# A two-layer graph transformer on one core: products of the seven-product blocks at the head of the next chunk, attention steps spread anew, two weight sums at other chunks

## The chip, the cores and the metric

The kernel runs on one core of a Trainium2 chip. The metric is the device time of one execution in microseconds (us); lower is better. Engines: TensorE (PE) multiplies matrices, VectorE (DVE), ScalarE (ACT) and GpSimd (POOL) do the rest, SyncE (SP) and the other queues issue DMAs. Each engine works its own instructions in the order in which the kernel gives them out and waits for the others through semaphores.

## What is computed

Two layers, one after the other, over 2708 nodes with 512 features, 8 heads and a 0/1 adjacency matrix with some nine ones in a row, the diagonal included. Each layer is

```
q, k, v = h @ Wq.T + bq, h @ Wk.T + bk, h @ Wv.T + bv        # 8 heads of 64
scores  = where(adj + eye == 0, -1e9, q.k / 8);  attn = softmax(scores)
h1 = layer_norm(h + (attn @ v) @ Wo.T + bo)
h2 = layer_norm(h1 + relu(h1 @ W1.T + b1) @ W2.T + b2)       # 512 -> 2048 -> 512
```

All of it is in float32.

## The kernel before, in words

The nodes are sorted by their number of neighbours and cut into 22 tiles of 128 (the last has 20). A tile gathers the keys and values of its neighbours slot by slot instead of forming the full score matrix. Tiles go in pairs called blocks; there are 11, k = 0 to 10, and the last holds the tile of 20 rows.

A layer is a loop over blocks, and in each block a loop over the 16 **chunks** f of the hidden 2048 features. A chunk is four matmuls into a PSUM tile pf (8 records in the profile, since a float32 matmul is recorded twice) and a relu on ACT into ft (L1656). Between two chunks the generator yields, and the driver loop puts other work in this gap, always at the same f:

- f = 5 to 8, "behind" (`keys_values`): the pair of the block before is turned for the next layer. f = 5: transposes of both tiles z (tp, L1285) and their copies zT on ACT (L1290). f = 6 and 7: one tile's k and v projection each (L620), k evicted by DVE (L1723), v by ACT (L1728). f = 8: two scatters to DRAM by POOL.
- f = 10, 11, 12, "attended": the next block's attention result cx. f = 10: transpose of the first tile and its copy cT on ACT. f = 11: first tile's output projection o, then the transpose of the second tile. f = 12: the second tile's o. Each o is followed on DVE by the residual, the bias and a layer norm (L1447 to L1279; its reciprocal root, L1275, is on POOL).
- f = 15: transposes of both normed tiles h, copies hT on ACT, for the next block's first chunk.
- in every gap, last: `advance(pace[f])` adds pace[f] to a credit (held at 1.5 at most) and issues steps of the **attention** of tiles further on while the credit is above zero. A step takes one or two neighbour slots: on DVE a product with q (L1150), a reduction (L1156) and two operations of an earlier step (L1182, L1189), some 4.3 us together; on ACT two exponentials (L1169) and eight scalings (L1176); on POOL two gathers, three steps ahead. A tile's last step is followed by eight divisions on ACT (cx, L1220).

Blocks 2 to 9 of layer 0 multiply ft by W2 in **seven products instead of eight** (`feed_forward_by_seven`). Chunks 2j and 2j+1 make pair j. Four small DVE operations form sums of the pair's ft (`sums`, L1617 to L1620), and seven matmuls of 256 columns (`products`, L1635) use them and sums of the weights, which lie in DRAM (form_d) and come back pair by pair (`ask_forms`, L1602, on SP). `sums(j)` is given out in chunk 2j+2, `products(j)` in chunk 2j+5. After chunk 15: the last pair but one, the last two chunks of ft by the plain way (L1665, L1669), products(6), and then DVE combines the accumulators into z (L1687 to L1695) and norms both tiles. The next block follows.

The sums of the weights are formed once, in block 1, on DVE (`form`, L1584 to L1587, four operations for each of seven pairs, then three stores by SP) in the gaps of the chunks listed in FORMS. Forms 0 to 5 use the same three buffers, so each waits until the stores of the one before have landed; form 6 has buffers of its own.

Four things set waits around the change. pf has two PSUM buffers, so chunk f waits for the relu of chunk f-2. The sums have two buffers, so `sums(j)` waits for `products(j-2)`. ACT's queue is strict: a copy that waits for TensorE holds up the relus behind it. Transposes and projections share two further PSUM buffers.

Of the kernel before, what the change touches and what calls it, by code (L numbers as in the profile page):

```python
# [51 lines left out]
    (0.0,) * 4 + (0.85,) * 8 + (0.0,) * 2 + (0.8,) * 2,  # L52
    (0.75,) * 11 + (0.0,) * 2 + (0.9,) * 3,
)
PACE7 = (0.0,) * 3 + (0.75,) * 2 + (1.2,) * 4 + (0.75,) * 2 + (0.0,) * 2 + (0.85,) * 3
FORMED = 1
FORMS = (3, 5, 7, 9, 13, 14, 15)
PACE = (
    (0.0,) * 2 + (0.6,) * 3 + (1.2,) * 4 + (0.6,) * 2 + (0.0,) * 2 + (0.8,) * 3,
    (0.0,) * 2 + (0.82,) * 9 + (0.0,) * 2 + (1.0,) * 3,  # L60
# [423 lines left out]
def by_edges(ctx: ExitStack, tc: tile.TileContext, x, xT, adj, layers, out, redo):  # L484
# [780 lines left out]
    def norm(z, r, gain, shift, st=None):  # L1265

        if st is None:
            st = small.tile([P, 6], F32, tag="st", name="st")
            nc.vector.bn_stats(st[:r], z[:r])
        mv = small.tile([P, 2], F32, tag="mv", name="mv")  # L1270
        nc.vector.bn_aggr(mv[:r], st[:r])
        va = small.tile([P, 1], F32, tag="va", name="va")
        nc.vector.tensor_scalar(va[:r], mv[:r, 1:2], EPS, None, ALU.add)  # L1273
        rd = small.tile([P, 1], F32, tag="rd", name="rd")
        nc.gpsimd.tensor_tensor(rd[:r], va[:r], mhalf[:r], ALU.pow)  # L1275
        nc.vector.scalar_tensor_tensor(
            z[:r], z[:r], mv[:r, 0:1], gain[:r], ALU.subtract, ALU.mult
        )
        nc.vector.scalar_tensor_tensor(z[:r], z[:r], rd[:r], shift[:r], ALU.mult, ALU.add)  # L1279
# [14 lines left out]
    class Layer:  # L1294
# [310 lines left out]
        def feed_forward_by_seven(self, k, block, hs, hT):  # L1605

            J, W = NFC // 2 - 1, 2 * P
            L, R = slice(0, W), slice(W, DM)
            a0, a1 = (ps_a.tile([P, DM], F32, tag=f"a{i}", name=f"a{i}") for i in range(2))
            c0, c1 = (ps_s.tile([P, DM], F32, tag=f"c{i}", name=f"c{i}") for i in range(2))  # L1610
            fts = []
            base = 3 * J * (k - FORMED - 1)

            def sums(j):
                f0, f1 = fts[2 * j], fts[2 * j + 1]
                s = self.sums[j % 2]
                nc.vector.tensor_tensor(s[:, 0], f1[:, P:], f0[:, P:], ALU.add)  # L1617
                nc.vector.tensor_tensor(f0[:, P:], f0[:, :P], f0[:, P:], ALU.subtract)
                nc.vector.tensor_tensor(s[:, 1], s[:, 0], f0[:, :P], ALU.subtract)
                nc.vector.tensor_tensor(s[:, 2], f1[:, :P], s[:, 1], ALU.subtract)  # L1620

            def products(j):
                f0, f1, w, s = fts[2 * j], fts[2 * j + 1], self.w2[j], self.sums[j % 2]
                t2, t3, t4 = self.slots
                first, last = j == 0, j == J - 1
                for to, left, right, start, stop in (
                    (a1[:, L], f1[:, P:], t4, first, last),
                    (c0[:, R], s[:, 1], t2, first, False),
                    (c1[:, L], f0[:, P:], t3, first, False),
                    (c0[:, L], f0[:, :P], w[:, 0, L], False, last),  # L1630
                    (a0[:, L], f1[:, :P], w[:, 1, L], first, False),
                    (c1[:, R], s[:, 0], w[:, 0, R], False, last),
                    (a0[:, R], s[:, 2], w[:, 1, R], False, last),
                ):
                    nc.tensor.matmul(to, left, right, start=start, stop=stop)  # L1635
                self.ask_forms(base + min(3 * j + 6, 3 * J + 3 * (k < NB - 2)))
                if k == NB - 2:
                    self.form_back(j)

            self.ask_forms(base + 3)  # L1640
            for f in range(NFC):
                j = f // 2
                pf = ps_f.tile([P, DM], F32, tag="f", name="pf")
                for c in range(NC):
                    nc.tensor.matmul(  # L1645
                        pf[:, :W],
                        self.w1[j][:, c, f % 2 * P : f % 2 * P + P],
                        hT[:, c, :],
                        start=(c == 0),
                        stop=(c == NC - 1),  # L1650
                    )
                if f % 6 < 4:
                    ft = dn.tile([P, W], F32, tag="ft", name="ft", bufs=4)
                else:
                    ft = self.more_fts[f % 2]
                nc.scalar.activation(ft, pf[:, :W], AF.Relu, bias=self.b1[:, f : f + 1])  # L1656
                fts.append(ft)
                if f % 2 == 0 and j > 0:
                    sums(j - 1)
                if f % 2 and j > 1:  # L1660
                    products(j - 2)
                yield None
            for i in range(2):
                f, w = 2 * J + i, self.w2[J]
                nc.tensor.matmul(a0, fts[f][:, :P], w[:, i, :], start=False, stop=False)  # L1665
            for cols in (L, R):
                for i in range(2):
                    f, w = 2 * J + i, self.w2[J]
                    nc.tensor.matmul(  # L1669
                        a1[:, cols],  # L1670
                        fts[f][:, P:],
                        w[:, i, cols],
                        start=False,
                        stop=False,
                    )
            products(J - 1)
            zA, zB = hs
            u2 = dn.tile([P, W], F32, tag="ft", name="u2", bufs=4)
            u34 = dn.tile([P, DM], F32, tag="row", name="u34", bufs=3)

            def twice(t):
                return t.unsqueeze(1).to_broadcast([P, 2, W])

            def pair(t):
                return t.rearrange("p (two n) -> p two n", two=2)

            nc.scalar.copy(u2, c0[:, L])  # L1687
            nc.vector.tensor_tensor(zA[:, L], u2, zA[:, L], ALU.add)
            nc.vector.tensor_tensor(u2, c0[:, R], u2, ALU.add)
            nc.vector.tensor_tensor(pair(u34), pair(c1), twice(u2), ALU.add)  # L1690
            nc.vector.tensor_tensor(zB[:, R], c1[:, R], zB[:, R], ALU.add)
            nc.vector.tensor_tensor(zA, a0, zA, ALU.add)
            nc.vector.tensor_tensor(zB, a1, zB, ALU.add)
            nc.vector.tensor_tensor(zA[:, R], u34[:, R], zA[:, R], ALU.add)
            nc.vector.tensor_tensor(pair(zB), pair(zB), twice(u34[:, L]), ALU.add)  # L1695
            for z in hs:
                norm(z, P, self.g2, self.e2)
            yield list(hs)
# [110 lines left out]
    def advance(more):  # L1809

        nonlocal credit
        if not more:
            return
        credit = min(credit + more, 1.5)
        while credit > 0 and len(got) < CXB:
            cost = next(ahead, None)
            if cost is None:
                break
            credit -= cost
# [49 lines left out]
    for n in range(NL):  # L1869
# [47 lines left out]
        for k, block in enumerate(blocks):  # L1917
# [14 lines left out]
            for f, zs in enumerate(working):  # L1932
# [16 lines left out]
                if more and f == NFC - 1:  # L1949
                    finish(asking)  # L1950
                    hT = now.turned(blocks[k + 1], hs_next)
                advance((PACE7 if seven else (PACE if k else PACES)[n])[f])
                if f in (0, 3, 7, 9) and (f or k):
# [4 lines left out]
                if n > 0 and (k, f) == (0, 2):  # L1958
                    now.load_second(1, temp)
                if n == 0 and k == FORMED and f in FORMS:  # L1960
                    now.form(FORMS.index(f))
                if last and not more and f == 8:
# [108 lines left out]
```

## Time and profile before

| What | us |
|---|---|
| median of 3 runs (1845.54 to 1848.74) | 1846.1 |
| profiled execution, its own time | 1845.1 |
| its span (first to last instruction) | 1843.4 |
| stretch of the seven-product blocks | 393 to 1020 |

Busy time by engine in stretches of the span, one to a block (the blocks' work straddles the cuts a little):

| stretch, us | length | PE busy | DVE busy | ACT busy |
|---|---|---|---|---|
| 392.0 to 472.0 (block 2) | 80.0 | 74.15 | 68.82 | 37.87 |
| 472.0 to 550.9 | 78.9 | 76.50 | 68.03 | 42.38 |
| 550.9 to 627.2 | 76.3 | 75.74 | 68.71 | 41.46 |
| 627.2 to 707.2 | 80.0 | 77.26 | 68.56 | 44.70 |
| 707.2 to 783.6 | 76.4 | 76.27 | 67.23 | 42.38 |
| 783.6 to 862.9 | 79.3 | 77.04 | 68.06 | 44.23 |
| 862.9 to 939.2 | 76.3 | 75.26 | 70.03 | 42.02 |
| 939.2 to 1020.0 (block 9) | 80.8 | 78.34 | 49.57 | 31.32 |

How to read it: busy time of PE counts matmuls whose ends are modelled, so the idle time in front of each matmul is the better measure. The profile names for each idle time the engine that ended it. Granted clock is the share of full speed that TensorE was given.

### The profile page before, as it was taken

Reading aid. Unit: us, or ns where it says so; the run is one execution under the profiler, and the core shown is the slowest. Engines: PE = TensorE matmul, PEld = TensorE weight load, DVE = VectorE, ACT = ScalarE, POOL = GpSimd, SP = SyncE. Lnnn points to the kernel's source line nnn. Section 1 sums busy time; section 2 is a strip of 40 time slices with the busy share of each in tenths; the row PEclk is TensorE's granted clock in tenths of the full one; section 3 lists DMA queues with packets and bytes.
Section 4 is the critical chain, followed back from the end, with each engine's and each line's share of the span. In section 5 each row is a group of like instructions: output and inputs, shape, how many; then the busy total and the mean of one; then the engine's idle time right before and its main releaser. Section 6 shows DMA issues by size and latency. Waiting matters only on the chain.

```text
span 1843.4 us, 22524 instructions
## 1 busy us (share of the span) xinstructions
PE 1812.7 (98%) x6563; PEld 1164.1 (63%) x6563; DVE 1460.4 (79%) x2447; ACT 950.5 (52%) x3271; POOL 799.4 (43%) x745
## 2 busy tenths in 40 slices
PE   9999999999999999999999999999999999999998
PEld 4444466566767867777677644666666666666666
DVE  5996778888888889889985247977988897889853
ACT  4770445545555555555643204565655675566531
POOL 3234755534454454444531022444554554456302
PEclk9999999999999999999999999999999999999999
DMA  9997987756666675665742677835554564555300
GB/s 340 365 347 257 371 279 237 245 166 228 205 222 206 206 258 191 215 200 192 244 161 90 231 247 276 314 124 197 193 192 174 207 249 150 210 195 184 135 20 21
DMA packets 158063, 393.82 MB, mean 214 GB/s; under 512 B 17515, under 2 KB 60895, under 8 KB 157929
## 3 DMA queue, kind: packets, MB, share of 16 engines
q0 software_dynamic: 70608, 252.12, 40.0%
q1 hardware_dynamic: 77162, 118.55, 18.7%
q10 hardware_dynamic: 10158, 21.61, 3.1%
q8 instruction: 54, 0.88, 0.2%
q14 instruction: 81, 0.66, 0.1%
HBM read 338.78 MB, written 53.44 MB: 213 GB/s over the span
## 4 chain that ended last, share of the span: by engine, by line
PE 82%; DVE 9%; ACT 4%; issue 3%; POOL 2%; DMA 1%; POOLq 0%; SPq 0%; DVEq 0%
PE pf L1515 18%; PE a L1488 17%; PE k L620 8%; PE v L620 8%; PE q L620 8%; PE o L620 7%; PE pf L1645 5%; PE c L1635 4%; PE a L1635 2%; PE tp L1285 2%; ACT kv L1176 2%; DVE sc L1156 2%; DVE kv L1150 1%; POOL rd L1275 1%; DVE h L1279 1%
## 5 line engine op out<-in xcount | busy, mean ns | idle before, releaser
L1113 POOL DMA_INDIRECT kv<-kv_d,listed x420 | 519.9, 1238 | 287.9 <-issue 114.4
L1515 PE MATMUL pf<-hT,w 128*128 128x256 f32 (+1 forms) x1792 | 393.3, 367 | 0.1
L1515 PEld LDWEIGHTS pf<-hT,w 128*128 128x128 f32 x1792 | 323.7, 190 | 103.0 <-issue 63.9
L1488 PE MATMUL a<-w,ft 128*128 128x512 f32 x800 | 373.2, 592 | 0.0
L1176 ACT ACTIVATE kv<-kv,p 128x64 f32<-128x64 f32 x1232 | 311.0, 335 | 5.0
L1275 POOL TENSOR_TENSOR rd<-va,mhalf 128x1 f32<-128x1 f32 (+1 forms) x88 | 80.7, 917 | 533.5 <-DVE va L1273 533.4
L1150 DVE TENSOR_TENSOR kv<-kv,q 128x1024 f32<-128x1024 f32 (+1 forms) x222 | 256.9, 1157 | 14.3 <-DMA q<-q_d,ident_i 11.0
L1156 DVE TENSOR_REDUCE sc<-kv 128x16 f32<-128x1024 f32 (+1 forms) x222 | 257.9, 1162 | 7.6
L1645 PE MATMUL pf<-hT,w 128*128 128x256 f32 x1024 | 235.1, 382 | 9.5 <-ACT ft L1656 9.5
L1189 DVE TENSOR_TENSOR acc<-acc,kv 128x1024 f32<-128x1024 f32 (+2 forms) x178 | 205.3, 1154 | 32.9 <-ACT kv L1176 17.3
L1645 PEld LDWEIGHTS pf<-hT,w 128*128 128x128 f32 x1024 | 193.3, 191 | 47.6 <-issue 11.9
L1488 PEld LDWEIGHTS a<-w,ft 128*128 128x128 f32 x800 | 150.3, 190 | 113.1 <-issue 101.2
L1526 ACT ACTIVATE ft<-pf,b 128x256 f32<-128x256 f32 (+1 forms) x208 | 94.8, 458 | 197.8 <-PE pf L1515 197.6
L1169 ACT ACTIVATE p<-sc,listed 128x8 f32<-128x8 f32 x420 | 104.3, 297 | 161.7 <-DVE sc L1156 150.8
L620 PE MATMUL o<-wo,cT 128*128 128x512 f32 x336 | 151.0, 593 | 1.1 <-ACT cT L1290 1.1
L1182 DVE TENSOR_TENSOR kv<-kv,p 128x512 f32<-128x512 f32 (+1 forms) x178 | 123.3, 693 | 9.8 <-ACT p L1169 9.6
L620 PEld LDWEIGHTS o<-wo,cT 128*128 128x128 f32 x336 | 63.5, 190 | 74.7 <-issue 66.2
L1656 ACT ACTIVATE ft<-pf,b 128x256 f32<-128x256 f32 x96 | 44.6, 466 | 114.1 <-PE pf L1645 114.1
L745 DVE MAX8 tops<-code 128x8 f32<-128x247 f32 (+2 forms) x242 | 78.9, 400 | 27.2 <-ACT code L740 27.0
L1279 DVE SCALAR_TENSOR_TENSOR h<-h,rd,ln_b 128x512 f32<-128x512 f32 (+1 forms) x88 | 66.1, 751 | 43.2 <-POOL rd L1275 43.2
L1220 ACT ACTIVATE cx<-acc,su 128x64 f32<-128x64 f32 (+1 forms) x352 | 88.2, 333 | 14.6 <-DVE su L1212 8.9
L1447 DVE TENSOR_TENSOR h<-o,xb 128x512 f32<-128x512 f32 (+1 forms) x44 | 30.3, 689 | 79.7 <-PE o L620 63.1
(231 smaller groups left out, 2332.0 us busy)
## 6 DMA issues: line engine op xcount, KB each, us to landing
aj<-in_adj SPq DMA_DIRECT2D x42, 677.0 KB, 6.2
forms<-form_d SPq DMA_DIRECT2D x168, 128.0 KB, 3.8
kv_d<-kvs ACTq DMA_DIRECT2D x21, 512.0 KB, 7.1
xg<-in_xT SPq DMA_DIRECT2D x19, 512.0 KB, 8.2
w<-in_W SPq DMA_DIRECT2D x16, 512.0 KB, 6.5
kv<-kv_d,listed POOLq DMA_INDIRECT x420, 6.0
zT_d<-zT SPq DMA_DIRECT2D x22, 256.0 KB, 3.5
xb_d<-h SPq DMA_DIRECT2D x21, 256.0 KB, 5.2
```

The costliest lines, as they stand in the source:

```text
L620: nc.tensor.matmul(o[:r], xs(c), wm[:, c, :], start=(c == 0), stop=(c == NC - 1))
L1113: return nc.gpsimd.indirect_dma_start(out=to, out_offset=None, in_=table[:, :], in_offset=bass.IndirectOffsetOnAxis(ap=s, axis=0), bounds_ ...
L1150: nc.vector.tensor_tensor(kv[:r, :c, :DM], kv[:r, :c, :DM], self.q[:r].unsqueeze(1).to_broadcast([r, c, DM]), ALU.mult,)
L1156: nc.vector.tensor_reduce(self.sc[:r, s0 : s0 + c, :], kv[:r, :c, :DM].rearrange("p s (h d) -> p s h d", d=DK), AX.X, ALU.add,)
L1169: nc.scalar.activation(p[:r, s, :], self.sc[:r, s, :], AF.Exp, bias=minus[:r, g, s : s + 1])
L1176: nc.scalar.activation(to[:, i, hd], kv[:r, i, DM + h * DK : DM + (h + 1) * DK], AF.Copy, scale=p[:r, s0 + i, h : h + 1],)
L1182: nc.vector.tensor_tensor(to[:, 0, :].rearrange("p (h d) -> p h d", d=DK), kv[:r, 0, DM:].rearrange("p (h d) -> p h d", d=DK), p[:r, s0, : ...
L1189: nc.vector.tensor_tensor(self.acc[:r, :c, :], self.acc[:r, :c, :], kv[:r, :c, DM:], ALU.add)
L1488: nc.tensor.matmul(a[:r, cols], fts[f][:, c0 : c0 + r], self.w2[f // 2][:, f % 2, cols], start=(f == 0), stop=(f == NFC - 1),)
L1515: nc.tensor.matmul(pf[:, :w], self.w1[f // 2][:, c, f % 2 * P : f % 2 * P + P], hT[:, c, :w], start=(c == 0), stop=(c == NC - 1),)
L1635: nc.tensor.matmul(to, left, right, start=start, stop=stop)
L1645: nc.tensor.matmul(pf[:, :W], self.w1[j][:, c, f % 2 * P : f % 2 * P + P], hT[:, c, :], start=(c == 0), stop=(c == NC - 1),)
```

## The change

Three edits, all in layer 0:

```
-PACE7 = (0.0,) * 3 + (0.75,) * 2 + (1.2,) * 4 + (0.75,) * 2 + (0.0,) * 2 + (0.85,) * 3
+PACE7 = (0.0,) * 4 + (0.6,) + (1.3,) * 4 + (0.6,) * 2 + (0.0,) * 2 + (0.5, 0.8, 2.4)
 FORMED = 1
-FORMS = (3, 5, 7, 9, 13, 14, 15)
+FORMS = (3, 5, 7, 9, 11, 13, 15)
...
                 if f % 2 == 0 and j > 0:
                     sums(j - 1)
+                yield None
                 if f % 2 and j > 1:
                     products(j - 2)
-                yield None
```

- **Products.** `products(j)` is given out after the gap of chunk 2j+5 instead of ahead of it, just before the matmuls of chunk 2j+6. On TensorE the gap's work of chunks 5, 7, 9, 11, 13 and 15 therefore comes before the seven products. The requests for the weight sums (`ask_forms`) and, in block 9, the requests that bring W2 back move with it on SP's queue, past the stores of zT and z in that gap.
- **Pace.** In blocks 2 to 9 the attention's credit by chunk is 0 to 3: nothing (before: nothing up to 2, then 0.75), 4: 0.6 (0.75), 5 to 8: 1.3 (1.2), 9 and 10: 0.6 (0.75), 11 and 12: nothing, 13: 0.5, 14: 0.8, 15: 2.4, of which at most 1.5 is held (before 0.85 each).
- **Weight sums.** Form 4 moves from chunk 13 to 11 of block 1 and form 5 from chunk 14 to 13.

## The prediction

> **What bounds the kernel now.** First the page's busy times: TensorE is busy nearly throughout, so only its idle time can be won. Then who ended that idle time between 392 and 1021 us, where the blocks that the edit touches lie (columns: total us, times, longest).
>
> ```profile
> PE   1812.7 (98%) x6563; PEld 1164.1 (63%) x6563; DVE 1460.4 (79%) x2447; ACT 950.5 (52%) x3271; POOL 799.4 (43%) x745
> ```
>
> ```profile
> PE pf L1645 <- ACT ft L1656: 9.5, 7, 2.2
> PE c L1635 <- issue: 3.1, 1, 3.1
> PE k L620 <- ACT zT L1290: 2.8, 5, 0.6
> PE c L1635 <- DVE forms L1619: 1.0, 1, 1.0
> PE a L1635 <- DVE h L1559: 0.8, 1, 0.8
> ```
>
> That is 17.2 us in 15 waits. The start-to-start times of the tail matmuls (L1665) hold all losses: 386.5 (the first chunk of block 2 at 393.0, less the tail and seven products, 6.5), 470.3, 548.8, 625.5, 705.9, 781.5, 860.5, 937.5 and 1013.8. A block without a wait is 75.45: 16 chunks at 1.73, 7 times 3.02 for seven products, four k or v at 3.43, two o, 2.6 of transposes, 3.44 of tail, at the pitches that the timeline shows (block 6: 75.6); block 9, whose o of 20 rows takes 1.0, is 72.9. Above that lie 8.3, 3.1, 1.2, 5.0, 0.1, 3.5, 1.5 and 3.4 us for blocks 2 to 9: **26.1 us is all that these edits can win.**
>
> The commonest loss, block 3's, on TensorE and then ACT:
>
> ```profile
> 518.10 0.59 PE L1635 MATMUL a<-w,forms 128*128 128x256 f32 x2
> 520.03 1.99 PE L1645 MATMUL pf<-hT,w 128*128 128x256 f32 x8 [1.34 <-ACT ft L1656]
> 521.86 0.60 PE L1285 MATMUL tp<-ident,cx 128*128 128x128 f32 x4
> 522.83 2.00 PE L1645 MATMUL pf<-hT,w 128*128 128x256 f32 x8 [0.36 <-ACT ft L1656]
> ```
>
> ```profile
> 512.25 0.58 ACT L1728 COPY kvs<-v 128x512 f32<-128x512 f32 x1 [9.41 <-PE v L620]
> ...
> 517.62 2.00 ACT L1220 ACTIVATE cx<-acc,su 128x64 f32<-128x64 f32 x8
> 519.52 0.46 ACT L1656 ACTIVATE ft<-pf,b 128x256 f32<-128x256 f32 x1
> ```
>
> ACT's queue stands at the copy of the second v until TensorE ends it. Then come two steps (2.45 each), the divisions (1.92), and only then the relu of chunk 8, for which chunk 10 waits. Between that v and chunk 10 TensorE has 6.5 us of other work.
>
> **Products after the gap.** It adds no instruction, only order. In block time (0 is the first chunk, 10.35 the end of chunk 5):
>
> - *Chunk 7.* Both of the second k and v now precede products(1), so ACT's copy is released 3.02 us earlier against chunk 10: v ends at 31.4, chunk 10 stands at 40.9. ACT by rows: v copy 32.0, a step 34.4, relu 8 when its chunk ends, 36.6, a step and the divisions 41.0, relu 9 at 41.4. Chunk 10 needs relu 8 and chunk 11, at 43.1, relu 9: both in time. In blocks 5 and 6 a second step precedes relu 9 in the new order: 43.8, a wait of 0.7 each. 9.5 becomes 1.4.
> - *Chunk 5.* The transposes of z come before products(0), so zT has 3.0 us more before k asks: the 2.8 go. That the relu of chunk 4 no longer stands behind a step of chunk 3 (the pace) helps too.
> - *What is late next, at chunk 11.* o of the first tile loses the cover of products(3). Relu 10 follows a step, 44.2, then four copies cT of 0.26: 45.25. o could start at 44.8. It waits 0.4 to 0.6 in blocks 2, 3, 4 and 7; in 5 and 6 chunk 11's own wait covers it. In block 9 relu 9 stands behind two steps and the divisions of tile 0: 2.9 if they wait for DVE as the durations have it, 1.5 if not. I take 2.9, since DVE is the later queue there.
> - *At chunk 15* the transposes of h lose the same 3.02. h is normed 4.3 us after the second o (536.91 to 541.24); then come two chunks, products(4) and another: 8.2 us, still covered. Without that cover one norm chain, 4.3, would show.
> - *SP.* The weight sums of the last pair are asked for when the first matmul of products(5) frees a buffer; 6.46 us lie between that and products(6), as much as between products(4) and (5) before, where no wait shows. The page has 3.8 us to landing. zT and z are ready by then, so nothing waits behind their stores: nothing. If that cover went, each late load would be a wait of its lateness.
>
> **z at chunk 5: the price.** The transposes of z now meet DVE without products(0) ahead. z is ready 9.95 us after its first operation (476.07 to 486.02), itself due some 13.1 us after chunk 14's start. From the end of the second o DVE has: norm 4.3, 0.6 until products(4) frees the sums, sums 1.1, two full steps 8.6, the closing step with its tile's sums 4.2, about 0.8 waiting for ACT, z 9.95: 29.6. TensorE from there to the second transpose of z: chunk 1.73, products 3.02, two chunks 3.45, transposes 0.87, products 3.02, tail 3.44, products 3.02, six chunks 10.35, 0.44: 29.3. So they meet within half a microsecond: I put 0.45 each on blocks 5, 6 and 8, nothing on 4 and 7 (a one-slot step), nothing on 9. Block 3 pays 1.85, since in block 2 a fourth step stands behind the second o. The wait does not build up: the second o holds DVE again in every block. Products(0) itself moves 0.87 later while its sums stay, so the 1.0 of block 8 goes.
>
> **Weight sums sooner.** Before, products(0) of block 2 stood still at 405.06, and the page says "issue"; DVE's timeline has its sum (L1619) at 407.71, the end of block 1's norms. DVE idled before both o of block 1 (2.85 and 2.89 us) and waited 0.81 for the stores in the last forms. Form 4 (1.76) now falls into the second idle time, and the store has four chunks more: z and the sums come 2.55 earlier, at 404.65. The transposes, asked at 403.5, wait 0.9; the 3.88 go.
>
> **Pace.** Ten to eleven steps a block as before. The step at chunk 3 moves behind; what it costs is in the three steps before z above.
>
> [...] The waits have a second price. The windows after the two longest waits:
>
> ```profile
> 408.00:412.00 4.00, 3.90 (x11) 3.20 (x12) 3.86 (x8) 0.00 (x0) 3.08 (x4) 0.62 0.71 223
> 678.00:682.00 4.00, 3.76 (x10) 3.03 (x11) 3.83 (x7) 3.90 (x16) 2.46 (x3) 0.58 0.94 329
> ```
>
> The column before the last two is the granted clock: 0.62 after an idle 3.06 and 0.58 after 2.18, where the chunk took 3.43 instead of 1.89. After idles of 1.98 and 1.90 it stayed 1.00. These slow stretches are some 1.75 and 1.5 us, 3.3 of the 26.1. [...]
>
> **The sum.** New waits: 0.9 + 0.6 (block 2), 1.85 + 0.4 (3), 0.4 (4), 0.45 + 0.7 (5), 0.45 + 0.7 (6), 0.4 (7), 0.45 (8), 2.9 (9) = 10.2. Twelve restarts at 0.1 (eight records take 1.99 after a wait, 1.89 without): 1.2. Clock once: 1.5. One norm's reciprocal root kept behind gathers on POOL, as at 848.13 (1.59 idle instead of 0.45): 1.1. Together 14.0 against 26.1: **12 us won**. The profiled execution, 1845.1, becomes 1833; the median shown, 1.0 above it, 1834. The rest, from 1020 us on, is moved forward unchanged: layer 1 hangs on block 10's keys, and TensorE waits there for 2 us in all.
>
> Bounds: if z is on time everywhere and block 9 waits 1.5 without a clock loss, new losses are 5.5 and the time 1825.5. If POOL's 1.1 falls on all seven blocks and two idles cost clock, 7.7 and 3.0 more: 1845.
>
> **Rivals.**
>
> - *The wait moves, half the gain.* o at cT waits 1.5 in each block, not 0.4, because steps on ACT are stretched by exponentials that wait for DVE (8.6 us and 20.7 us of such waits now, on either side), and z some 0.4 more: 6 us less won, 1840. For it: both meetings above are within half a microsecond. Against: ACT is busy 42 of 76 us and idles 9 us before that v.
> - *Slower: z becomes the bound.* Should DVE be 2.5 us later at z than worked out in each of seven blocks, TensorE waits 17.5 us more at chunk 5, and these idles, at 2.5 to 3, cost 1.5 of clock each, 10.5: 1834 + 28 = 1862. It decides from about 1.5 us of lateness per block (10.5 takes the gain away). For it: DVE is busy 68 to 70 of 76 us, and 1.95 us of such lateness stood at 868.25 in block 7. Against: in six of eight blocks z waited for ACT's copy now, 0.2 to 1.3 us and 10.3 in the last, and the second o resets the queue.
> - *Only block 2 gains.* If the order of the products is hidden anyway, the 3.88, the clock after it and a little remain: 1840.5. Against: the waits for the relus are TensorE's own idle time, on the chain of waits.
>
> **How the numbers follow.** My forecast, 1834 with its own range 1829 to 1839: 0.68. Half the gain or block 2 only, about 1840: 0.24, of which a quarter lies above 1842.4. Slower: 0.08. Some 0.2% (3.7 us) is what a measurement tells from no change. Faster: 0.68 + 0.18 = 0.86; within: 0.06 and 0.01 of the last; slower 0.07. The range runs from 1828 to 1843, with 0.1 left above and a little below.
>
> **What would show it.** Right: no wait of pf on ft over 1 us; none of k on zT; waits of o on cT of about half a microsecond; transposes of z waiting for DVE by less than 2 us; products(0) of block 2 by about 406; the tail's start-to-start near 76.3; the stage ending near 1008. Wrong: z's transposes waiting 2 us or more in most blocks with windows of clock near 0.6, or the forms' loads ending waits of products(6).

## The result, and the profile after

| | before | after |
|---|---|---|
| median, us (range, 5 runs each) | 1846.7 (1845.5 to 1848.7) | 1836.6 (1834.3 to 1838.4) |
| ratio of times, 95% interval | | 0.9945 (0.993 to 0.9959) |
| profiled execution, its own time | 1845.1 | 1835.8 |
| its span | 1843.4 | 1834.1 |
| first chunk of block 2 to the tail of block 9 | 393.00 to 1013.78: 620.78 | 394.26 to 1004.77: 610.51 |

The last row is the measure used from here on, called **the stretch**: from the first record of L1645 of block 2 to the first of L1665 of block 9. It became 10.27 us shorter. That it began 1.26 later in this execution lies ahead of the blocks measured (TensorE waited 1.17 for DVE at 151 us, for one), and differs between the kept traces: 392.84 to 394.51. The change won 10 us, where 12 were predicted.

The busy times hardly tell the two kernels apart. The columns are busy us, share of the span and instructions:

```profile
PE 1809.1 (99%) x6563; PEld 1163.0 (63%) x6563; DVE 1458.5 (80%) x2447; ACT 948.7 (52%) x3271; POOL 798.9 (44%) x745
```

The waits of TensorE between 385 and 1015 us do (total us, times, longest). This is the whole list:

```profile
PE tp L1285 <- DVE h L1279: 3.9, 6, 1.6
PE pf L1645 <- ACT ft L1656: 3.8, 3, 2.2
PE o L615 <- ACT cT L1290: 2.4, 1, 2.4
PE a L1635 <- DMA forms<-form_d: 0.4, 1, 0.4
```

17.2 us of waits have become 10.5. The relus fell from 9.5 to 3.8, and k's waits for zT and those for the sums are gone. In their place stand the transposes of z, which now meet DVE at chunk 5, and one wait of o. Block 3 after, the place of the commonest loss before; ACT, then TensorE (start, us, instruction):

```profile
511.92 2.00 ACT L1220 ACTIVATE cx<-acc,su 128x64 f32<-128x64 f32 x8
513.83 0.45 ACT L1656 ACTIVATE ft<-pf,b 128x256 f32<-128x256 f32 x1
...
516.99 1.11 ACT L1290 ACTIVATE cT<-tp,bv 128x128 f32<-128x128 f32 x4
```

```profile
513.46 0.59 PE L1635 MATMUL a<-w,forms 128*128 128x256 f32 x2
513.89 1.89 PE L1645 MATMUL pf<-hT,w 128*128 128x256 f32 x8
515.62 0.60 PE L1285 MATMUL tp<-ident,cx 128*128 128x128 f32 x4
516.05 1.89 PE L1645 MATMUL pf<-hT,w 128*128 128x256 f32 x8
517.78 2.74 PE L620 MATMUL o<-wo,cT 128*128 128x512 f32 x6
```

The divisions still stand ahead of a relu, but the products now stand ahead of chunk 10 on TensorE, and no bracket follows either L1645: nothing waited. o, too, starts at 517.78 without a wait, while the four copies cT last until 518.10: its first matmuls do not wait for all four.

What the prediction did not have is in block 8. POOL, DVE and then TensorE (in brackets the idle time before, and who ended it):

```profile
882.33 1.75 POOL L1113 DMA_INDIRECT kv<-kv_d,listed  x1 [9.68 <-DVE acc L1189]
884.38 1.51 POOL L1113 DMA_INDIRECT kv<-kv_d,listed  x1 [0.30 <-issue]
886.19 0.99 POOL L1113 DMA_INDIRECT kv<-kv_d,listed  x1 [0.30 <-issue]
887.48 1.61 POOL L1113 DMA_INDIRECT kv<-kv_d,listed  x1 [0.30 <-issue]
889.40 1.00 POOL L1113 DMA_INDIRECT q<-q_d,ident_i  x1 [0.30 <-issue]
```

```profile
889.15 0.20 DVE L1212 RECIPROCAL su<-su 128x8 f32<-128x8 f32 x1
894.76 1.22 DVE L1150 TENSOR_TENSOR kv<-kv,q 128x1024 f32<-128x1024 f32 x1 [5.41 <-DMA q<-q_d,ident_i]
```

```profile
900.22 1.99 PE L1645 MATMUL pf<-hT,w 128*128 128x256 f32 x8 [2.24 <-ACT ft L1656]
```

Read upwards: chunk 11 waited 2.24 for the relu of chunk 9. On ACT that relu, at 899.72, stood behind the exponentials and scalings of a step, which began at 897.27 because DVE's product with q began at 894.76. DVE had been idle since 889.35, because the gather of q was issued at 889.40; and that gather stood on POOL behind four gathers of keys and values, the first of which had waited 9.68 us for a free buffer.

The granted clock fell once, to 0.50 for 3.41 us, around the end of the wait of o in block 9. (Columns: start and end, length, busy time of TensorE with its records, granted clock, DMA share, GB/s. A stretch of 4 us across the edge shows a mean, 0.68 from 980 to 984.)

```profile
978.05:981.46 3.41, 1.00 (x8) 1.00 0.00 0
981.46:984.88 3.42, 3.42 (x14) 0.50 0.02 5
```

### The profile page after: what moved, and what is told of

Its sections match the earlier page's. It is cut to its first block, busy times and chain, and to the rows that moved or that the text cites. A ratio compares the mean times of both kernels' runs of the same rounds, so it can differ in the third digit from the quotient of the medians.

```text
span 1834.1 us, 22527 instructions
## 1 busy us (share of the span) xinstructions
PE 1809.1 (99%) x6563; PEld 1163.0 (63%) x6563; DVE 1458.5 (80%) x2447; ACT 948.7 (52%) x3271; POOL 798.9 (44%) x745
## 4 chain that ended last, share of the span: by engine, by line
PE 81%; DVE 10%; ACT 3%; issue 3%; DMA 2%; POOL 1%; POOLq 0%; DVEq 0%; ACTq 0%
PE pf L1515 17%; PE a L1488 16%; PE q L620 8%; PE o L620 8%; PE pf L1645 7%; PE k L620 7%; PE v L620 7%; PE c L1635 4%; PE a L1635 3%; PE tp L1285 2%; DVE sc L1156 2%; DVE kv L1150 2%; ACT kv L1176 1%; POOL rd L1275 1%; DVE acc L1189 1%
## 5 line engine op out<-in xcount | busy, mean ns | idle before, releaser
L1645 PE MATMUL pf<-hT,w 128*128 128x256 f32 x1024 | 233.2, 379 | 3.8 <-ACT ft L1656 3.8
L1645 PEld LDWEIGHTS pf<-hT,w 128*128 128x128 f32 x1024 | 193.9, 190 | 37.8 <-issue 7.9
```

The costliest lines, as they stand in the source:

```text
L1645: nc.tensor.matmul(pf[:, :W], self.w1[j][:, c, f % 2 * P : f % 2 * P + P], hT[:, c, :], start=(c == 0), stop=(c == NC - 1),)
```

## The experiments

**1. Which part won what.** Three kernels make one part alone, and one leaves the pace out. Each is the kernel before with the lines named:

```
e1_products   products(j) behind the gap's yield; PACE7 and FORMS as before
e2_pace       PACE7 new; products and FORMS as before
e3_forms      FORMS new; products and PACE7 as before
e4_old_pace   products and FORMS new; PACE7 as before
```

> Only the products move behind the gap; pace and weight sums as before. Measure: the stretch from the first chunk of block 2 to the tail of block 9, 620.8 us before and 610.5 changed. Theory A (the parts need each other: the old pace leaves ACT and DVE steps in chunk 3, so zT stays late and the second k then waits for DVE to evict the first, since products(1) no longer stands between them): 618 to 621, the waits of pf for its relu mostly gone, but waits of k of 0.5 to 3.5 us and of o for cT of 1.4 and 2.6 in their place, z's transposes wait 3 us only in block 2. Rival B (moving the products is the whole effect): near 613, and this kernel within 2 us of the full change.

> Only the attention's pace changes; products ahead of the gap, weight sums as before. Theory A (the new pace puts three steps before z, so products(0) waits for its sums in each block, by 1.3 to 3.3 us, with clock lost after the longer ones): slower than before, the stretch 630 to 640 us against 620.8, time up by 8 to 20 us. Rival B (the pace itself brings the gain, by taking the step out of chunk 3): faster, the stretch below 616.

> Only the two weight sums move, the rest as before. Theory A: products(0) of block 2 wait 1.8 us instead of 3.9, too short to lose clock: the stretch 4 to 4.5 us shorter, 616.5; no other wait changes. Rival B (DVE is late in block 2 for another reason than the order of its sums, the wait called issue stays at 3 us): no change, 620.8.

> The full change with the old pace: products behind the gap and weight sums sooner. Theory A: block 2 gains its 6 us, the later blocks trade waits for relus against waits of k and o as in the run with the products alone: the stretch 614 to 617, between before and the full change. Rival B (the pace does nothing): 610.5, as the full change.

| | stretch, us | time, us (runs) | ratio to before (95%) |
|---|---|---|---|
| before | 620.8 | 1847.0 (13) | 1 |
| products alone | 614.6 | 1840.9 (7) | 0.9964 (0.9952 to 0.9977) |
| pace alone | 641.8 | 1866.7 (4) | 1.0106 (1.0089 to 1.0123) |
| weight sums alone | 617.1 | 1841.0 (7) | 0.9964 (0.9953 to 0.9975) |
| products and sums | 613.5 | 1836.6 (4) | 0.9938 (0.9922 to 0.9955) |

The parts do not add. The pace alone costs 21 us of the stretch, and here is where (TensorE's waits, 390 to 1045 us, the two largest):

```profile
PE c L1635 <- DVE forms L1619: 18.9, 7, 3.2
PE pf L1645 <- ACT ft L1656: 8.2, 5, 2.2
```

In the old order products(0) come at the end of chunk 5 and ask for their sums, which stand on DVE's queue behind z and its norms. The new pace puts more of the steps ahead of z: in block 3 z's first operation (L1688) starts 9.16 us after the tail (478.49 and 469.33), where it was 5.77 before (476.07 and 470.30). So TensorE stands still for about 2.7 us in each of seven blocks. All its waits together are 31.0 us against 17.2, and the clock fell seven times instead of twice. The new order of the products lets the transposes of z go first, which need less of that queue. The pace pays only with the products. With the products alone the stretch, 614.6, lies nearer to the rival's 613 than to the 618 to 621 of my theory: the waits for k (5.9 us in all) and for z in block 2 (2.9) came, but o waited 2.6, not 4.0. The rival's other sign failed too: the time, 1840.9, is 4.3 above that of the change.

Products and sums without the pace (waits as above, the six largest):

```profile
PE o L620 <- ACT cT L1290: 2.6, 2, 2.1
PE k L620 <- issue: 2.3, 4, 0.6
PE k L620 <- ACT kvs L1728: 2.2, 1, 2.2
PE tp L1285 <- DVE h L1279: 0.9, 1, 0.9
PE k L620 <- ACT zT L1290: 0.9, 1, 0.9
PE pf L1645 <- ACT ft L1656: 0.8, 1, 0.8
```

The relus' 9.5 are gone with the old pace too: that gain is the products'. But k still waits 5.4 in these rows. The four waits at issue, some 0.56 each, are the old wait for zT under another name. Block 3 of this run, TensorE and then ACT:

```profile
482.15 1.04 PE L1285 MATMUL tp<-ident,h 128*128 128x128 f32 x8
488.50 3.70 PE L620 MATMUL k<-wk,zT 128*128 128x512 f32 x8 [0.56 <-issue]
```

```profile
485.05 2.02 ACT L1176 ACTIVATE kv<-kv,p 128x64 f32<-128x64 f32 x8
486.98 0.45 ACT L1656 ACTIVATE forms<-pf,b 128x256 f32<-128x256 f32 x1
487.34 2.14 ACT L1290 ACTIVATE zT<-tp,bo 128x128 f32<-128x128 f32 x8
```

z was turned by 483.19, but ACT had a step and a relu ahead of the copies, and k began when the first tile's four were done. In the change the same copies begin at 484.76. The new pace takes this wait away and pays with z's transposes, the gather of q and o in block 9.

**2. Is the pace worth anything?** The whole change and the one without the pace again, in five rounds side by side:

> The full change once more, beside the one with the old pace on the same chip. Theory A (the pace is worth the 3 us by which the two profiled stretches differ, 610.5 against 613.5): 3 us faster than the old pace. Rival B (the pace is worth nothing as it stands, its gain on k and o given back through the late q): within 1.5 us of it.

> The full change with the old pace once more. Theory A: 1839 to 1840, the full change at 1836 to 1837. Rival B: both at 1836 to 1838.

The whole change took 1838.3 us, ratio 0.9939 (0.9927 to 0.9952), stretch 612.9; without the pace it took 1837.5, ratio 0.9928 (0.9915 to 0.994), stretch 612.0. The rival was right: no worth of the new pace as it stands can be told from the noise.

**3. Would cover at chunk 5 pay?** Only products(0) go back ahead of the gap:

```
+                if f % 2 and j > 1 and (f == 5):
+                    products(j - 2)
                 yield None
-                if f % 2 and j > 1:
+                if f % 2 and j > 1 and not (f == 5):
                     products(j - 2)
```

> The full change, but products(0) of each block stay ahead of the gap of chunk 5; all other products behind their gaps. Measure: the stretch from the first chunk of block 2 to the tail of block 9, 610.5 us in the full change. Theory A (DVE is what arrives late at chunk 5: products(0) need the sums that follow z on DVE, so the wait only changes its name and grows by the 0.9 of z's transposes that stand ahead of the products no longer): no wait of z's transposes, products(0) wait for DVE's sums by 0.2 to 2.7 us in every block, together about 9.5 us instead of 3.9; the stretch 616 to 620. Rival B (it is the order on TensorE that makes the transposes wait): 606, the 3.9 us gone.

No. The time was 1840.5 (4 runs), ratio 0.995 (0.9933 to 0.9966), not told from the change's 0.9945 and 0.9939. The stretch was 621.0, over the 616 to 620 expected, but its execution was by far the slowest of the four (1845.9; the others 1838.8 to 1840.7): the clock fell three times in it, and chunk 11 of block 8 waited 3.7. The waits of z's transposes are gone, and this stands in their place (1.7 more, in block 2, ended at issue):

```profile
PE c L1635 <- DVE forms L1619: 6.4, 6, 2.4
PE pf L1645 <- ACT ft L1656: 5.3, 3, 3.7
```

The wait at chunk 5 belongs to DVE's queue, not to z: whatever TensorE asks of DVE there comes late, and the sums of products(0) come later than z.

**4. How near is the slower rival?** One of the operations that make z is given out five times, with the same result each time, so that z is ready some 2.45 us later in every block:

```
             nc.vector.tensor_tensor(pair(u34), pair(c1), twice(u2), ALU.add)
+            nc.vector.tensor_tensor(pair(u34), pair(c1), twice(u2), ALU.add)
+            nc.vector.tensor_tensor(pair(u34), pair(c1), twice(u2), ALU.add)
+            nc.vector.tensor_tensor(pair(u34), pair(c1), twice(u2), ALU.add)
+            nc.vector.tensor_tensor(pair(u34), pair(c1), twice(u2), ALU.add)
```

> The full change with one operation on the way to z (0.61 us apart) given out five times instead of once: z is 2.45 us later in each block, nothing else is changed and the numbers stay as they are. Theory A (z is on the critical path with at most 0.5 us to spare, and an idle of over 2 us lowers the granted clock): waits of z's transposes of 2.0 to 3.0 us in blocks 3 to 9 (4.1 in block 3), about 16 us more in all, and 1.5 us of clock for most of them: the stretch 628 to 637, time up by 18 to 27 us. [...] Rival C (DVE has time to spare before the transposes): under 615.

The time was 1864.0 (4 runs), ratio 1.0087 (1.007 to 1.0103): slower than before. The stretch was 634.8, 24.3 longer than that of the change.

```profile
PE tp L1285 <- DVE h L1279: 21.1, 13, 2.2
```

17.2 of the 24.3 are the growth of this row, and 7.1 are left, mostly for clock and restarts: the clock fell four times, in the change once. Block 3 shows both, first the windows (granted clock third from the end), then TensorE:

```profile
484.00:488.00 4.00, 1.79 (x10) 1.47 (x9) 3.38 (x11) 2.64 (x11) 2.63 (x3) 0.88 0.00 0
488.00:492.00 4.00, 4.00 (x14) 3.28 (x14) 3.83 (x7) 1.47 (x7) 3.39 (x3) 0.69 0.89 260
```

```profile
483.79 0.66 PE L1285 MATMUL tp<-ident,h 128*128 128x128 f32 x4 [2.15 <-DVE h L1279]
486.65 0.80 PE L1285 MATMUL tp<-ident,h 128*128 128x128 f32 x4 [2.21 <-DVE h L1279]
487.25 1.06 PE L1635 MATMUL a<-forms,ft 128*128 128x256 f32 x2
...
490.56 0.59 PE L1635 MATMUL a<-w,ft 128*128 128x256 f32 x2
```

A product takes 1.06 instead of 0.59 until 490.5. The rival said 17.5 of waits and 10.5 of clock. Its mechanism was right and its clock too dear by a third at least; 2.45 us of lateness on DVE in each block turn 10.3 us won into 14.0 lost (634.8 against 620.8 before). Nor did every wait of this length lose clock: of the ten of 2.04 to 2.41 us in this trace four did, and of the eight among them that were z's transposes three, where the expectation set 1.5 us for most.

**5. Mending the two late waits.** The query of the last tile is asked for one tile sooner, together with that of the tile before it, so that its gather no longer stands behind those that wait for buffers. The second kernel has the second part of this diff too: products(3) of block 9 go back ahead of the gap of chunk 11, as cover for o:

```
                 if q is None and g != order[-1]:
                     q = asked(n, order[order.index(g) + 1])
+                    if n == 0 and g == order[-3]:
+                        own[order[-1]] = asked(n, order[-1])
...
+                if f % 2 and j > 1 and ((k, f) == (NB - 2, 11)):
+                    products(j - 2)
                 yield None
-                if f % 2 and j > 1:
+                if f % 2 and j > 1 and not ((k, f) == (NB - 2, 11)):
                     products(j - 2)
```

> The full change, with the rows of q for the last tile in the order asked for with those of the tile before it, ahead of POOL's gathers of keys that wait for buffers. Theory A (the 5.4 us for which DVE waited for that q held back the step whose exponentials stand before the relu of chunk 9 on ACT, and so made chunk 11 of block 8 wait 2.24 us): both waits go, the stretch 608 to 608.5, time 1 to 3 us down; block 9's wait of o for cT, 2.4 us, stays. Rival B (ACT's queue alone makes the 2.24): it stays, 610.5.

> As the run with q sooner, and products(3) of block 9 alone stand ahead of their gap again, between chunk 11 and o of its first tile. Theory A (o waits since it lost the cover of the products, 3.0 us against a wait of 2.4, and the idle lowers the clock by about 2 us): the wait and the clock loss go, the stretch 603.5 to 605, time 1829 to 1833. Rival B (the copies cT are late by more than the products cover, or the products wait themselves for their sums): less than 2 us gained over the run with q sooner.

With q sooner the time was 1830.8 (1830.3 to 1831.2, 4 runs), ratio 0.99 (0.9884 to 0.9917), stretch 606.4, two more won than the 608 expected at best. DVE's wait for q and chunk 11's wait in block 8 are both gone, which shows the chain read in the profile after. The wait of o in block 9 stayed, 2.41, but this execution lost no clock behind it, some 1.6 us of the excess; the last section has how often a wait of this length did. With the cover as well it was **1827.3** (1826.1 to 1828.9, 4 runs), ratio 0.9879 (0.9863 to 0.9896), stretch 603.9, below the time expected. TensorE's waits in it, the whole list:

```profile
PE tp L1285 <- DVE h L1279: 3.6, 5, 1.7
PE pf L1645 <- ACT ft L1656: 1.6, 2, 0.8
PE c L1635 <- DMA forms<-form_d: 1.2, 2, 0.8
```

o waits no more, and 6.4 us are left of 10.5. This version beats both kernels.

**6. The pace again, with both mends.** The last kernel with the old PACE7:

> The full change with q sooner and products(3) of block 9 ahead of their gap, but with the old pace. Theory A (the new pace is worth its gain on k, zT and o once the late q and the cover are mended): the waits of k (about 5.5 us) and of o for cT (2.6 us) of the old pace stay, the stretch 612 to 614 against 603.9 with the new pace, time 1834 to 1838 against 1827.3. Rival B (mending these two is the whole gain whatever the pace): 604 to 606, 1827 to 1829.

The time was 1837.1 (6 runs), ratio 0.9941 (0.9927 to 0.9954), stretch 612.5, as without the mends: under the old pace k and o wait where they did (k at issue 2.3 and for ACT's v copy 2.2, o 2.6). So the new pace is worth 8.6 us of the stretch, but only once q and o of block 9 are mended. Some 3.2 of the 8.6 are clock: it fell twice in this trace, behind the waits of k and o, and never in that of the last kernel (1.6 each, as worked out below).

## Why the prediction was nearly right, by its own steps

- **The relus, 9.5 to 1.4: right in blocks 3 to 7, wrong in block 8.** Blocks 5 and 6 wait 0.79 each, 0.7 was said. The 2.24 of block 8 are the step that failed: the prediction worked out ACT's queue by durations alone and let every step begin in time. DVE's 5.41 for q was not in it. That a gather of q may stand on POOL behind gathers that wait for buffers was nowhere weighed; experiment 5 shows what it cost: block 8 lasts 76.10 with q sooner, against 78.60 and, in the second execution, 80.70.
- **Transposes of z, the price: right.** Measured 0.86, 1.65, 0, 0.29, 0.29, 0, 0.42 and 0.44 in blocks 2 to 9, predicted 0.9, 1.85, 0, 0.45, 0.45, 0, 0.45 and 0: 3.9 against 4.1. Experiment 4 confirms how near the edge this lies.
- **o on cT: right in block 9 (2.4 against 2.9), too large elsewhere.** The 0.4 to 0.6 in each of blocks 2, 3, 4 and 7, 1.8 in all, did not come. In blocks 2, 3 and 7 the last copy was as late as said, 0.66, 0.32 and 0.53 after o's start, but o does not wait for it; in block 4 the copies were in time. In the second execution o waited 1.08 in block 2, after ACT had stood still for 0.99 ahead of the copies.
- **k on zT, 2.8 to nothing: right in size, wrong in cause.** It was put down mostly to the order of the products, which gives zT 3.0 us more. With that order and the old pace ACT makes zT as late as before, and k waits 5.4. It is the pace, named there as a help, that clears it.
- **Pace: no term of its own, which was the weakest step.** Alone it costs 21 us of the stretch, with the products nothing, with the two mends it gives 8.6 (clock included). It came out right for the sum by accident: its gain on k and its losses on z, q and o cancel.
- **Weight sums: right.** Products(0) of block 2 start at 406.58, against 406 said. Alone this part shortens the stretch by 3.7.
- **SP: nearly right.** One load of forms is 0.4 late in block 4 where nothing was said.
- **Clock once, 1.5: right in size, with luck in the count.** In block 9 the start of o to the first c product takes 3.98 us, and 2.39 where the same wait cost no clock (the kernel with q sooner): 1.6. That it fell there was not settled by the length of the wait, as the prediction's reading of the rows had it: the last section.
- **Sum.** New waits: 10.2 said, 10.5 measured, of another make-up. Clock 1.5 and 1.6. Of the 26.1 us of loss 26.1 - 10.27 = 15.8 remain; 15.8 - 10.5 - 1.6 = 3.7 are left for restarts and POOL, where 2.3 were put. No row tells these last ones apart.
- **Signs named beforehand.** The tail's start-to-start is 77.2 on average, not 76.3, and the stage ends at 1011, not 1008. No pf wait over 1 us: one, in block 8. Half the gain, 1840, the likeliest rival, lies 3.5 us above the result; its mechanism, o waiting 1.5 in each block, did not occur.

## What to carry to other kernels

Two schedules that meet in one queue can't be priced one by one: a pace that costs 21 us alone was neutral beside the new order and worth 8.6 us after two small mends, so an edit of two parts wants a run of each and of both. When work is moved from behind a wait, list what each queue holds at that moment, the queue that issues gathers too: a request that is needed soon may stand behind requests that wait for buffers. Where the cover of a wait is taken away everywhere, look for the one place where it was still needed and leave it there.

## What the runs showed of the hardware

The clock's price of a wait did not follow from its length alone. Two executions of the change have a profile. In the first, block 9's wait of 2.40 lost clock (shown above), and block 8's wait of 2.24 did not. In the second it was the other way round: block 8's wait, 2.65 there, lost clock, and block 9's 2.41 did not.

```profile
903.02 2.67 PE L1645 MATMUL pf<-hT,w 128*128 128x256 f32 x8 [2.65 <-ACT ft L1656]
...
984.68 1.53 PE L615 MATMUL o<-wo,cT 128*20 128x512 f32 x8 [2.41 <-ACT cT L1290]
```

Eight records of pf took 2.67 instead of 1.99, and those of o took 1.53 where they had taken 2.28. Block 8 of the second execution lasted 80.70 against 78.60, block 9 76.28 against 78.56.

Around these two waits the second execution reads so (engines, granted clock, DMA share and GB/s as in experiment 4). The first row holds block 8's wait, the last two hold block 9's:

```profile
900.00:904.00 4.00, 1.35 (x9) 1.01 (x8) 3.79 (x9) 3.90 (x16) 2.10 (x2) 1.00 0.30 61
904.00:908.00 4.00, 4.00 (x9) 2.38 (x8) 3.83 (x11) 3.37 (x15) 3.08 (x4) 0.57 0.85 278
980.00:984.00 4.00, 2.26 (x12) 1.67 (x12) 3.18 (x11) 1.92 (x8) 0.00 (x0) 1.00 0.00 0
984.00:988.00 4.00, 3.32 (x19) 2.18 (x20) 1.69 (x3) 2.62 (x11) 0.00 (x0) 1.00 0.01 4
```

Between 385 and 1015 us the clock fell to 0.50 twice before, at 408.99 and 678.64, and once after, at 981.46, each time for 3.41 us. Over all thirteen profiles, these are TensorE's single waits between 385 and 1045 us from 1.3 us up, and how many had slow records right behind them (as the 1.06 instead of 0.59 of experiment 4):

| length of the wait, us | waits | with slow records behind them |
|---|---|---|
| 1.34 to 1.69 | 11 | 0 |
| 1.90 to 1.98 | 6 | 1 |
| 2.04 to 2.41 | 27 | 14 |
| 2.60 to 3.70 | 11 | 10 |

So a wait of 2.04 to 2.41 us lost clock in about half of all cases (14 of 27 = 0.52). Their length does not tell these from the others: a wait of 2.41 lost clock twice in the kernel of experiment 3, and not in the kernel with q sooner. Half speed for 3.41 us is 1.7 us of work, near the 1.6 measured in block 9. An author does best to price such a wait by its chance.
